# A transformer layer whose instruction order a planner writes: new durations and due times in the plan

## The chip, the core and the metric

The kernel runs on one core of one Trainium2 chip, in float32. Times are device microseconds (us) from the start of the program to its end. The profiler records one execution; its span goes from the first to the last instruction.

## What is computed

Eight sequences of 256 tokens with 512 features go through one layer. It normalises each token, runs causal attention with 32 query heads over 8 key/value heads of width 128 (so that 4 query heads share a key/value head), and multiplies the result by a gate from four small experts of which the best two count:

```python
xn = _layernorm(x)
q, k, v = heads of xn @ wq.T, xn @ wk.T, xn @ wv.T     # 32, 8 and 8 heads of 128
q, k = rotated by position                             # q * cos + rotate_half(q) * sin
scores = q @ k.T / sqrt(128)
scores = scores * scale        # for queries from position 107 on: 0.5 for keys under 35, 1.5 up to 107
probs = softmax(scores + causal)
s = (probs @ v) @ wo.T
g = silu(sum over the two best experts of gate * (xn @ A.T) @ B.T * 4)
return x + s * g
```

## The kernel before

**Blocks of work.** The tokens are cut into 4 token blocks (tb) of two sequences. Each block takes 8 steps, one for each key/value head with its 4 query heads (g). A step has two *units*, one for each sequence (b). A unit is one softmax: 4 heads x 256 queries x 256 keys.

The large products are done in Strassen-Winograd form: seven products of half matrices (pieces p1 to p7, four matmuls each) instead of eight, with sums and differences on VectorE before and after. `quad` makes the queries, keys and values in this way (TensorE tiles pa, pd, pe), `out_project` the output product (po). `out_project`'s left factors are the attention tiles a and their sums s; its results are added into acc by VectorE.

**A unit, link by link** (`softmax`, L681, and `values`, L806). TensorE writes the scores in three groups of query rows, 7-6, 5-4-3 and 2-1-0 (tiles sc). VectorE reduces each row to its least negated score (z, least). ScalarE takes the exponentials and their sums (p, total), with p one single buffer for all units, which the transposes of the unit before set free. VectorE then takes the reciprocal and scales p in two jobs (`scale`), and transposes 32x32 blocks in two more (`transpose`, tile blocks). SP, which issues transfers, writes these blocks to DRAM with four transfers (`spread`, there<-blocks) and reads them back with one (`gather`, pT<-there), so that the probabilities lie transposed for TensorE. Only then can TensorE multiply them by the values (`values`, tiles av, 6 matmuls in two pieces), ScalarE copy av to a, and `out_project` go on. The values of a unit come one step after its scores (LAG_V = 2 units).

**Who sets the order.** Nothing in the program waits for a scheduler at run time: each engine works through its instructions in the order in which the Python code issues them, and waits where an input is late. That order comes from `Plan` (L170). Each job is declared with `add` (L181): its engine, a duration in us, the jobs it comes after, the buffers it opens and closes (`Hold`, `Room`), a due time relative to a TensorE piece (`near`), and a `lag` for what passes until a transfer lands. TensorE's pieces are laid in a row by `lay` (L191), in the order that the loop at the end of `layer` (L1165 on) writes out. `Plan.run` (L195) gives every other job a due time: from `near`, or earlier where a job that needs it is due earlier. It then walks through its own clock. Whenever an engine is free by that clock, it takes the job with the earliest due time among those whose inputs are ready and whose buffers are free, and issues it; the job counts as done after its duration, the `lag`, and `HOP` (L175) for the signal. TensorE's pieces too are taken in this way: one that isn't ready by the plan's clock is passed by a later one. So a duration in the plan never makes an instruction longer or shorter; it moves instructions against each other.

**The start and the last steps.** `norm` (L309) loads four tiles of x per token block and finds mean and variance on VectorE (st, mv), the root on ScalarE and the reciprocal on VectorE (rstd), the normalised tile on VectorE (xn), its transpose on TensorE (xp) and a copy on ScalarE (XB). Weights come through GpSimd's queue (w, wo); in the first token block VectorE makes their sums, which are kept in DRAM for the later blocks. In the step loop each step's pieces are two lists, `fill` and `later`: scores and values of unit 0 and 1 (sa, va, sb, vb), and the output pieces of the step before (ob) and those held back from the one before that (oa). When no projection is left to weave in (the last steps), `fill + later` is laid as it stands.

Of the kernel before, what the change touches and what calls it, by code (L numbers as in the profile page):

```python
# [63 lines left out]
MIX = (SYS + IMG) // BLK  # L64
# [105 lines left out]
class Plan:  # L170
# [3 lines left out]

    HOP = 0.1  # L175
    AHEAD = 30.0
# [80 lines left out]
def layer(ctx: ExitStack, tc: tile.TileContext, x, wquad, woquad, raT, bT, table, out):  # L257
    nc = InOrder(tc)
# [50 lines left out]
    def norm(tb):  # L309
# [61 lines left out]
        for t in range(NT):  # L371
# [4 lines left out]
        loads = [  # L376
            add("dma", 0.0, lambda: None, after=[issues[t]], lag=6.0 if tb else 3.0 + 1.7 * t)
            for t in range(NT)
# [10 lines left out]
        for t in range(NT):  # L389
            xn = add("dve", 0.4, lambda t=t: normalise(t), after=[done[t]], opens=[mh[t]], closes=[xh[t // 2]])  # L390
            tp = add("pe", 0.5, lambda t=t: turn(t), after=[xn, identity], opens=[ph[t]], closes=[mh[t]])
            opens = [x_hold[tb]] if t == 0 else []
            after = [tp] + reads[:1]
            reads.append(
                add("act", 0.6, lambda t=t: read(t), after=after, opens=opens, closes=[ph[t]],
                    near=(tp, 0.5))
            )
            pieces.append(tp)
        t1 = add("dve", 0.7, lambda: add_up(0), after=reads)
        t2 = add("dve", 0.7, lambda: add_up(1), after=[t1])  # L400
        t3 = add("dve", 0.7, lambda: add_up(2), after=reads)
        t4 = add("dve", 0.7, lambda: add_up(3), after=[t2])
        acts[tb, "B"], acts[tb, "T"] = reads, [t1, t2, t3, t4]
# [4 lines left out]
    def blocks_of(tb, room, ring, source, kept, key, form, first):  # L408
# [26 lines left out]
        if tb:  # L435
            for i in order:
                after = [sums_of[room, key, i]] if i in form.sums else []
                there[i] = add("pool", 0.8, lambda i=i: load(i), after=after, opens=[holds[i]], lag=4.5)
            return box, holds, there
        issue = list(first)  # L440
        for i in order[:4]:
            there[i] = add(
                "sp" if first else "pool", 0.4 if first else 0.8, lambda i=i: load(i), after=issue,
                opens=[holds[i]], lag=10.0 if first else 4.5,
            )
        for i, (to, a, b, op) in enumerate(form.steps):
            there[to] = add(
                "dve", 0.7, lambda i=i: sum_up(i), after=[there[a], there[b]] + form.before(i, there),
                opens=[holds[to]] if to in order[4:] else [], closes=[holds[a], holds[b]],
            )  # L450
# [35 lines left out]
    def quad(tb, which, out, room, rows, name):  # L486
# [43 lines left out]
        def copy(what, p, h):  # L530
            return add(
                "act", 0.6, lambda: aside(what, "pa"), after=[p], opens=[h], near=(p, 0.0)
            )
# [5 lines left out]
        if not tb:  # L539
# [4 lines left out]
        o00 = add(  # L544
            "dve", 0.7, lambda: sum_up(0, 0, "pe", "p1"), after=[p2, c1], opens=[outs[0]],
            closes=[pe, s1], near=(p2, 1.0),
# [6 lines left out]
        o11 = add(  # L553
            "dve", 0.7, lambda: sum_up(1, 1, "pd", "u3"), after=[p5, c7], opens=[outs[1]],
            closes=[s3], near=(p7, 1.0),
        )
        p4 = piece("pa", A22, 0, 0, 3, False, [c7])
        o01 = add(
            "act", 0.6, lambda: nc.scalar.copy(out(0, 1), box["pa"]), after=[p4, o00],
            closes=[pa], near=(p4, 0.0),  # L560
        )
        p3 = piece("pd", S4, 1, 1, None, False, [o11])
        o10 = add(
            "dve", 0.7, lambda: sum_up(1, 0, "pd", "u2"), after=[p3, c6], closes=[pd, s2],
            near=(p3, 1.0),
# [3 lines left out]
    def rope(src, of, dst, opens, after, name):  # L569
# [21 lines left out]
        def turn():  # L591
            nc.vector.tensor_mul(split(box["sw"]), split(box["sw"]), wide(C_SIN))

        s0 = add("act", 1.05, lambda: swap(0), after=after, opens=[h], closes=[of])
        s1 = add("act", 1.05, lambda: swap(1), after=[s0], closes=[of])
        c = add(
            "dve", 1.22, lambda: nc.vector.tensor_mul(dst(), split(src()), wide(C_COS)),
            after=after + [tables], opens=opens, closes=[of],
        )
        t = add("dve", 1.22, turn, after=[s1])  # L600
        return add(
            "dve", 1.22, lambda: nc.vector.tensor_add(dst(), dst(), split(box["sw"])),
            after=[c, t], closes=[h],
# [12 lines left out]
    def keys_of(tb, half):  # L616

        pieces, outs, done, src = turned_quad(tb, KQ + half, f"k{tb}_{half}")

        def of(b):  # L620
            n = f"k{tb}_{half}_{b}"
            h, box = hold("kk"), {}

            def dst():
                if not box:
                    box["k"] = three.tile([P, G, 3, P], F32, tag="kk", name=f"k{n}")
                return box["k"][:, :, ::2, :]
# [9 lines left out]
            keys[tb, half, b] = box, h, add("dve", 0.7, rescale, after=[r])  # L637

        for b in range(NB):
            of(b)  # L640
        return pieces
# [39 lines left out]
    def softmax(tb, g, b):  # L681
# [93 lines left out]
        for rows in groups:  # L775
# [5 lines left out]
            red = add(  # L781
                "dve", sum(0.12 + 0.035 * (i + 1) for i in rows) + 0.3 * (MIX in rows),
                lambda r=rows: reduce(r), after=[sc], opens=[zh], closes=[sh], near=(sc, 1.0),
            )
            exps.append(
                add("act", sum(0.47 + 0.024 * (i + 1) for i in rows),
                    lambda r=rows: exponentials(r), after=[red, cleared] + exps[:1], closes=[zh],
# [15 lines left out]
        probs[tb, g, b] = box, th, in_  # L803
        return pieces

    def values(tb, g, b):  # L806
# [6 lines left out]
        def of(k):  # L813
# [18 lines left out]
            av = add("pe", 1.3, work, after=[p_done] + v_done, opens=[h], closes=[ph, vh])  # L832
            a = add("act", 0.6, read, after=[av], opens=[ah], closes=[h], near=(av, 1.0))
            attn[tb, g, b, k] = box, ah, a
# [6 lines left out]
    def out_project(tb, g):  # L841
# [19 lines left out]
        for i, (to, a, b, op) in enumerate(Features.steps):  # L861
            a_done[to] = add(
                "dve", 0.7, lambda i=i: sum_up(i),
                after=[a_done[a], a_done[b]] + Features.before(i, a_done),
# [4 lines left out]
        def product(k, a, w):  # L869
# [27 lines left out]
            mine["done"] = add(  # L897
                "act" if g == 0 else "dve", 0.7, add_up, after=[p, mine["done"]], closes=[h],
                opens=[mine["hold"]] if g == 0 else [], near=(p, 1.0),
# [17 lines left out]
    def finish(tb):  # L917
        M = {k: acc[tb, k] for k in range(1, 8)}

        def put(to, a, b, closes=()):  # L920
            near = max((M[a]["last"], M[b]["last"]), key=lambda p: p.number)
            M[to]["done"] = add(
                "dve", 0.7, lambda: nc.vector.tensor_add(M[to]["s"], M[a]["s"], M[b]["s"]),
                after=turn + [M[to]["done"], M[a]["done"], M[b]["done"]], closes=[M[k]["hold"] for k in closes],
# [8 lines left out]
        def inputs(b):  # L933
# [6 lines left out]
            def load(what):  # L940
# [6 lines left out]
                add("sp", 0.3, lambda: load("g"), after=gates[tb][2 * b : 2 * b + 2], opens=[xh],  # L947
                    near=near, lag=5.0),
                add("sp", 0.3, lambda: load("xf"), opens=[gh], near=near, lag=5.0),
            ]  # L950
            loads[b] = box, [xh, gh], done

        def result(k, b, f):
# [5 lines left out]
            m = add(  # L959
                "dve", 0.7, lambda: nc.vector.scalar_tensor_tensor(  # L960
                    s(), s(), 0.5, box["g"][:, :, cols], op0=ALU.mult, op1=ALU.mult
# [3 lines left out]
            a = add(  # L965
                "dve", 0.7, lambda: nc.vector.tensor_add(s(), s(), box["xf"][:, :, cols]),
                after=[m, done[1]], closes=[holds[1]], near=(near, 4.0),
# [22 lines left out]
    def experts(tb):  # L990
# [73 lines left out]
        p2 = add("pe", 0.5, turn, after=[r3], opens=[th])  # L1064
        last = add("act", 0.6, read, after=[p2], closes=[th], near=(p2, 0.5))

        def silu(t):
# [20 lines left out]
            p = add("pe", 0.86, work, after=[last], opens=[dh])  # L1088
            a = add("act", 0.6, half, after=[p], opens=[h], near=(p, 1.0))
            d = add("dve", 0.7, whole, after=[a], closes=[dh], near=(p, 2.0))  # L1090
            gates[tb].append(
# [73 lines left out]
    for n in range(len(steps) + 2):  # L1165
# [9 lines left out]
        if not last:  # L1175
# [51 lines left out]
```

## Time and profile before

| | |
|---|---|
| median of 3 runs | 1392.16 us (1383.55 to 1392.40) |
| profiled execution | 1394.26 us |
| its span | 1391.5 us |
| TensorE busy | 1340.2 us, 96% of the span |
| TensorE's weight loads | 1175.7 us, 84% |
| VectorE busy | 1102.4 us, 79% |
| ScalarE busy | 614.2 us, 44% |
| GpSimd busy | 313.8 us, 23% |
| moved by DMA | 275.8 MB, 198 GB/s mean |

PE is TensorE, DVE VectorE, ACT ScalarE, POOL GpSimd, SP SyncE; a q behind the name is the engine's queue, where transfers are issued. Names are the program's tiles, out<-in. The matmuls' ends are modelled by the profiler, so "busy" doesn't mean that TensorE is at its peak. In the view of waits a row gives who waited for whom, the us in total, how often, and the longest. In the timeline a row gives the start and the length in us, what ran and how often; in brackets, how long the engine was idle before it and what ended that. In the view by stretches a row gives the stretch, its length, the busy us of TensorE, of its weight loads, of VectorE, ScalarE and GpSimd (each with its number of instructions), the granted TensorE clock as a share of full speed, the share of DMA engines' time, and GB/s. Every line number is L118, since all instructions go through one recording helper; groups are told apart by their tiles.

### The profile page before, as it was taken

The numbers are of one execution on the slowest core, as the hardware profiler recorded it, in microseconds if no ns is written. First come the engines' busy times: TensorE is split into PE (matmuls) and PEld (weight loads), VectorE is DVE, ScalarE is ACT, GpSimd is POOL, SyncE is SP. The second block draws the span as 40 slices with busy tenths as digits, with TensorE's granted clock in tenths as the row PEclk, the third lists the DMA queues.
The fourth block names the chain that finished last, engine by engine and source line by source line (L and its number), as shares of the span: only waits on it lengthen the run. The fifth ranks groups of instructions, "written<-read, shape, count | busy, mean of one in ns | idle before, by whom it ended". The sixth has DMA issues, their size and how long they took to land.

```text
span 1391.5 us, 19888 instructions
## 1 busy us (share of the span) xinstructions
PE 1340.2 (96%) x6512; PEld 1175.7 (84%) x6512; DVE 1102.4 (79%) x2822; ACT 614.2 (44%) x1587; POOL 313.8 (23%) x579
## 2 busy tenths in 40 slices
PE   6999999999999999999999999999999999999985
PEld 5878888887888888888889888888878988888874
DVE  4897889898887868679687886868868877776885
ACT  2555444443544435345434554445543454444420
POOL 1422323222222122221222212212122121221110
PEclk9999999999999999999999999999999999999998
DMA  4676766666756666676667666666556586664672
GB/s 152 196 224 206 238 195 224 208 226 180 239 179 206 208 201 190 196 233 182 199 181 226 205 197 192 200 206 217 176 179 203 176 251 188 189 212 152 195 214 86
DMA packets 106134, 275.80 MB, mean 198 GB/s; under 512 B 15985, under 2 KB 52849, under 8 KB 106033
## 3 DMA queue, kind: packets, MB, share of 16 engines
q0 software_dynamic: 45760, 149.98, 34.7%
q1 hardware_dynamic: 59520, 123.76, 28.7%
q8 instruction: 52, 0.85, 0.2%
q10 hardware_dynamic: 752, 0.80, 0.2%
q14 instruction: 50, 0.40, 0.1%
HBM read 194.79 MB, written 79.69 MB: 197 GB/s over the span
## 4 chain that ended last, share of the span: by engine, by line
PE 83%; DMA 10%; DVE 4%; SPq 1%; issue 1%; ACT 0%; DVEq 0%; ACTq 0%
PE po L118 23%; PE paq L118 13%; PE av L118 11%; PE sc L118 9%; PE pdq L118 7%; DMA pT<-there 6%; PE pak L118 4%; PE pav L118 4%; DMA there<-blocks 4%; PE peq L118 3%; PE pdk L118 2%; PE pdv L118 2%; DVE acc L118 1%; PE dle L118 1%; PE pev L118 1%; PE lme L118 1%
## 5 line engine op out<-in xcount | busy, mean ns | idle before, releaser
L118 ACT ACTIVATE p<-z,least 128x256 f32<-128x256 f32 (+7 forms) x512 | 207.5, 407 | 110.6 <-DVE least L118 75.3
L118 PE MATMUL po<-wo,a 128*128 128x256 f32 x1024 | 241.2, 380 | 1.4 <-ACT a L118 1.4
L118 PE MATMUL av<-pT,v 128*128 128x256 f32 x768 | 194.1, 393 | 25.3 <-DMA pT<-there 25.3
L118 PEld LDWEIGHTS po<-wo,a 128*128 128x128 f32 x1024 | 192.2, 190 | 26.0 <-ACT a L118 2.6
L118 DVE CUSTOM_DVE_ANT_0 z<-sc,tab 128x256 f32<-128x256 f32 (+7 forms) x512 | 135.5, 301 | 78.8 <-PE sc L118 70.9
L118 PEld LDWEIGHTS av<-pT,v 128*128 128x128 f32 x768 | 149.5, 197 | 50.7 <-issue 14.4
L118 PE MATMUL po<-wo,s 128*128 128x256 f32 x768 | 182.7, 382 | 0.0
L118 PE MATMUL paq<-XT,w 128*128 128x256 f32 x768 | 182.0, 380 | 0.0
L118 PEld LDWEIGHTS sc<-kk,qTq 128*128 128x128 f32 x1024 | 159.9, 191 | 13.4 <-DVE least L118 1.0
L118 PE MATMUL sc<-kk,qTq 128*128 128x256 f32 (+7 forms) x1024 | 169.0, 303 | 1.3 <-DVE least L118 0.8
L118 DVE TENSOR_TENSOR acc<-acc,po 128x512 f32<-128x512 f32 x196 | 132.9, 678 | 46.7 <-PE po L118 44.8
L118 ACT COPY a<-av 128x512 f32<-128x512 f32 x128 | 73.9, 581 | 213.0 <-PE av L118 213.0
L118 PEld LDWEIGHTS po<-wo,s 128*128 128x128 f32 x768 | 145.2, 191 | 24.1 <-issue 5.3
L118 PEld LDWEIGHTS paq<-XT,w 128*128 128x128 f32 x768 | 144.8, 190 | 20.5 <-ACT p L118 0.8
L118 POOL DMA_DIRECT2D w<-sums x144 | 78.9, 548 | 361.0 <-PE paq L118 139.3
L118 ACT COPY swq<-cq 64x1024 f32<-64x1024 f32 x128 | 133.7, 1044 | 28.8 <-DVE qTq L118 22.7
L118 POOL DMA_DIRECT2D w<-in_wquad_dram x148 | 81.0, 549 | 252.4 <-PE paq L118 87.8
L118 DVE STREAM_TRANSPOSE blocks<-p 128x1024 f32<-128x1024 f32 (+1 forms) x128 | 123.5, 967 | 0.2
L118 DVE TENSOR_SCALAR p<-p,total 128x256 f32<-128x256 f32 (+7 forms) x512 | 118.1, 293 | 2.3
L118 ACT ACTIVATION_READ_ACCUMULATOR p<-z,least 128x1 f32 x512 | 96.1, 188 | 0.0
L118 DVE TENSOR_TENSOR qTq<-cq,tab 128x1024 f32<-128x1024 f32 x64 | 77.9, 1218 | 22.9 <-ACT cq L118 22.9
L118 POOL DMA_DIRECT2D wo<-osums x96 | 52.5, 546 | 152.5 <-PE po L118 152.5
(116 smaller groups left out, 1832.5 us busy)
## 6 DMA issues: line engine op xcount, KB each, us to landing
there<-blocks SPq DMA_DIRECT2D x256, 192.0 KB, 3.6
pT<-there SPq DMA_DIRECT2D x64, 768.0 KB, 5.7
w<-in_wquad_dram POOLq DMA_DIRECT2D x148, 256.0 KB, 4.7
w<-sums POOLq DMA_DIRECT2D x144, 256.0 KB, 3.8
wo<-in_woquad_dram POOLq DMA_DIRECT2D x104, 256.0 KB, 4.4
wo<-osums POOLq DMA_DIRECT2D x96, 256.0 KB, 4.2
sums<-w POOLq DMA_DIRECT2D x48, 256.0 KB, 3.6
osums<-wo POOLq DMA_DIRECT2D x32, 256.0 KB, 4.7
```

Source lines behind the costliest of these rows:

```text
L118: ins = what(*args, **kwargs)
```

## The change

The durations in the plan are set to new values, the due times of scaling, transposes and spread move nearer to the unit's last score piece, and the last step's pieces are laid in another order. No instruction is added, removed or altered. The same replacements as below are made wherever the old values stand: VectorE's sums 0.7 to 0.61, ScalarE's copies 0.6 to 0.5.

```diff
-    HOP = 0.1
+    HOP = 0.18
...
-            add("dma", 0.0, lambda: None, after=[issues[t]], lag=6.0 if tb else 3.0 + 1.7 * t)
+            add("dma", 0.0, lambda: None, after=[issues[t]], lag=8.5 if tb else 5.0 + 1.3 * t)
...
-                there[i] = add("pool", 0.8, lambda i=i: load(i), after=after, opens=[holds[i]], lag=4.5)
+                there[i] = add("pool", 0.8, lambda i=i: load(i), after=after, opens=[holds[i]], lag=6.0)
...
-        t = add("dve", 1.22, turn, after=[s1])
+        t = add("dve", 1.14, turn, after=[s1])
...
-                "dve", sum(0.12 + 0.035 * (i + 1) for i in rows) + 0.3 * (MIX in rows),
+                "dve", sum(0.06 + 0.033 * (i + 1) for i in rows) + 0.45 * (MIX in rows),
...
-                add("act", sum(0.47 + 0.024 * (i + 1) for i in rows),
+                add("act", sum(0.285 + 0.027 * (i + 1) for i in rows),
...
-        s0 = add("dve", 1.2, lambda: scale((7, 6, 5)), after=exps, near=(sc, 5.0))
-        s1 = add("dve", 0.9, lambda: scale((4, 3, 2, 1, 0)), after=[s0], near=(sc, 6.0))
+        s0 = add("dve", 0.95, lambda: scale((7, 6, 5)), after=exps, near=(sc, 3.0))
+        s1 = add("dve", 0.92, lambda: scale((4, 3, 2, 1, 0)), after=[s0], near=(sc, 3.5))
         t0 = add(
-            "dve", 1.24, lambda: transpose(False), after=[s1], opens=[bh], closes=[ph],
-            near=(sc, 7.0),
+            "dve", 1.17, lambda: transpose(False), after=[s1], opens=[bh], closes=[ph],
+            near=(sc, 4.0),
         )
         t1 = add(
-            "dve", 0.66, lambda: transpose(True), after=[t0], closes=[ph], near=(sc, 8.0)
+            "dve", 0.6, lambda: transpose(True), after=[t0], closes=[ph], near=(sc, 4.5)
         )
-        out_ = add("sp", 1.4, spread, after=[t1], closes=[bh], near=(sc, 9.0), lag=4.0)
-        in_ = add("sp", 0.35, gather, after=[out_], opens=[th], lag=5.0)
+        out_ = add("sp", 2.4, spread, after=[t1], closes=[bh], near=(sc, 5.0), lag=3.4)
+        in_ = add("sp", 0.35, gather, after=[out_], opens=[th], lag=7.0)
...
-                    near=near, lag=5.0),
-                add("sp", 0.3, lambda: load("xf"), opens=[gh], near=near, lag=5.0),
+                    near=near, lag=9.0),
+                add("sp", 0.3, lambda: load("xf"), opens=[gh], near=near, lag=9.0),
...
         later = [piece for some in later for piece in some]
+        if n == len(steps) - 1:
+
+            fill, later = sa + sb, oa + va + vb + ob[:2]
         main = []
```

More of the change, by code (lines that the diff above doesn't have):

```diff
@@ L394, in norm @@
             reads.append(
-                add("act", 0.6, lambda t=t: read(t), after=after, opens=opens, closes=[ph[t]],
+                add("act", 0.5, lambda t=t: read(t), after=after, opens=opens, closes=[ph[t]],
                     near=(tp, 0.5))
@@ L398, in norm @@
             pieces.append(tp)
[L399 to L402, printed above, removed]
+        t1 = add("dve", 0.61, lambda: add_up(0), after=reads)
+        t2 = add("dve", 0.61, lambda: add_up(1), after=[t1])
+        t3 = add("dve", 0.61, lambda: add_up(2), after=reads)
+        t4 = add("dve", 0.61, lambda: add_up(3), after=[t2])
         acts[tb, "B"], acts[tb, "T"] = reads, [t1, t2, t3, t4]
@@ L443, in blocks_of @@
                 "sp" if first else "pool", 0.4 if first else 0.8, lambda i=i: load(i), after=issue,
-                opens=[holds[i]], lag=10.0 if first else 4.5,
+                opens=[holds[i]], lag=10.0 if first else 6.0,
             )
@@ L447, in blocks_of @@
             there[to] = add(
-                "dve", 0.7, lambda i=i: sum_up(i), after=[there[a], there[b]] + form.before(i, there),
+                "dve", 0.61, lambda i=i: sum_up(i), after=[there[a], there[b]] + form.before(i, there),
                 opens=[holds[to]] if to in order[4:] else [], closes=[holds[a], holds[b]],
@@ L531, in copy @@
             return add(
-                "act", 0.6, lambda: aside(what, "pa"), after=[p], opens=[h], near=(p, 0.0)
+                "act", 0.5, lambda: aside(what, "pa"), after=[p], opens=[h], near=(p, 0.0)
             )
@@ L544, in quad @@
         o00 = add(
-            "dve", 0.7, lambda: sum_up(0, 0, "pe", "p1"), after=[p2, c1], opens=[outs[0]],
+            "dve", 0.61, lambda: sum_up(0, 0, "pe", "p1"), after=[p2, c1], opens=[outs[0]],
             closes=[pe, s1], near=(p2, 1.0),
@@ L553, in quad @@
         o11 = add(
-            "dve", 0.7, lambda: sum_up(1, 1, "pd", "u3"), after=[p5, c7], opens=[outs[1]],
+            "dve", 0.61, lambda: sum_up(1, 1, "pd", "u3"), after=[p5, c7], opens=[outs[1]],
             closes=[s3], near=(p7, 1.0),
@@ L558, in quad @@
         o01 = add(
-            "act", 0.6, lambda: nc.scalar.copy(out(0, 1), box["pa"]), after=[p4, o00],
+            "act", 0.5, lambda: nc.scalar.copy(out(0, 1), box["pa"]), after=[p4, o00],
             closes=[pa], near=(p4, 0.0),
@@ L563, in quad @@
         o10 = add(
-            "dve", 0.7, lambda: sum_up(1, 0, "pd", "u2"), after=[p3, c6], closes=[pd, s2],
+            "dve", 0.61, lambda: sum_up(1, 0, "pd", "u2"), after=[p3, c6], closes=[pd, s2],
             near=(p3, 1.0),
@@ L592, in turn @@
             nc.vector.tensor_mul(split(box["sw"]), split(box["sw"]), wide(C_SIN))
-        s0 = add("act", 1.05, lambda: swap(0), after=after, opens=[h], closes=[of])
-        s1 = add("act", 1.05, lambda: swap(1), after=[s0], closes=[of])
+        s0 = add("act", 1.0, lambda: swap(0), after=after, opens=[h], closes=[of])
+        s1 = add("act", 1.0, lambda: swap(1), after=[s0], closes=[of])
         c = add(
-            "dve", 1.22, lambda: nc.vector.tensor_mul(dst(), split(src()), wide(C_COS)),
+            "dve", 1.14, lambda: nc.vector.tensor_mul(dst(), split(src()), wide(C_COS)),
             after=after + [tables], opens=opens, closes=[of],
         )
-        t = add("dve", 1.22, turn, after=[s1])
+        t = add("dve", 1.14, turn, after=[s1])
         return add(
-            "dve", 1.22, lambda: nc.vector.tensor_add(dst(), dst(), split(box["sw"])),
+            "dve", 1.14, lambda: nc.vector.tensor_add(dst(), dst(), split(box["sw"])),
             after=[c, t], closes=[h],
@@ L636, in of @@
             r = rope(lambda: src[b], outs[b], dst, [h], done[b], n)
-            keys[tb, half, b] = box, h, add("dve", 0.7, rescale, after=[r])
+            keys[tb, half, b] = box, h, add("dve", 0.61, rescale, after=[r])
         for b in range(NB):
@@ L832, in of @@
             av = add("pe", 1.3, work, after=[p_done] + v_done, opens=[h], closes=[ph, vh])
-            a = add("act", 0.6, read, after=[av], opens=[ah], closes=[h], near=(av, 1.0))
+            a = add("act", 0.5, read, after=[av], opens=[ah], closes=[h], near=(av, 1.0))
             attn[tb, g, b, k] = box, ah, a
@@ L862, in out_project @@
             a_done[to] = add(
-                "dve", 0.7, lambda i=i: sum_up(i),
+                "dve", 0.61, lambda i=i: sum_up(i),
                 after=[a_done[a], a_done[b]] + Features.before(i, a_done),
@@ L897, in product @@
             mine["done"] = add(
-                "act" if g == 0 else "dve", 0.7, add_up, after=[p, mine["done"]], closes=[h],
+                "act" if g == 0 else "dve", 0.61, add_up, after=[p, mine["done"]], closes=[h],
                 opens=[mine["hold"]] if g == 0 else [], near=(p, 1.0),
@@ L922, in put @@
             M[to]["done"] = add(
-                "dve", 0.7, lambda: nc.vector.tensor_add(M[to]["s"], M[a]["s"], M[b]["s"]),
+                "dve", 0.61, lambda: nc.vector.tensor_add(M[to]["s"], M[a]["s"], M[b]["s"]),
                 after=turn + [M[to]["done"], M[a]["done"], M[b]["done"]], closes=[M[k]["hold"] for k in closes],
@@ L959, in result @@
             m = add(
-                "dve", 0.7, lambda: nc.vector.scalar_tensor_tensor(
+                "dve", 0.61, lambda: nc.vector.scalar_tensor_tensor(
                     s(), s(), 0.5, box["g"][:, :, cols], op0=ALU.mult, op1=ALU.mult
@@ L965, in result @@
             a = add(
-                "dve", 0.7, lambda: nc.vector.tensor_add(s(), s(), box["xf"][:, :, cols]),
+                "dve", 0.61, lambda: nc.vector.tensor_add(s(), s(), box["xf"][:, :, cols]),
                 after=[m, done[1]], closes=[holds[1]], near=(near, 4.0),
@@ L1064, in experts @@
         p2 = add("pe", 0.5, turn, after=[r3], opens=[th])
-        last = add("act", 0.6, read, after=[p2], closes=[th], near=(p2, 0.5))
+        last = add("act", 0.5, read, after=[p2], closes=[th], near=(p2, 0.5))
         def silu(t):
@@ L1088, in silu @@
             p = add("pe", 0.86, work, after=[last], opens=[dh])
-            a = add("act", 0.6, half, after=[p], opens=[h], near=(p, 1.0))
-            d = add("dve", 0.7, whole, after=[a], closes=[dh], near=(p, 2.0))
+            a = add("act", 0.5, half, after=[p], opens=[h], near=(p, 1.0))
+            d = add("dve", 0.61, whole, after=[a], closes=[dh], near=(p, 2.0))
             gates[tb].append(
```

## The prediction

> **What bounds the kernel now.** I read the chain of work that ended last first, for the engine that sets the end; then the waits, for what TensorE lacks; then the stretches around single waits, for what a wait costs after it is over; then the timelines of one late softmax, for which step made it late.
>
> ```profile
> PE 83%; DMA 10%; DVE 4%; SPq 1%; issue 1%; ACT 0%; DVEq 0%; ACTq 0%
> ```
>
> TensorE sets the end. The 10% of DMA is 6% gathers of the turned probabilities (pT<-there) and 4% spreads of their blocks: the last links of softmax, which TensorE waits for before it can multiply by the values. The waits:
>
> ```profile
> PE av L118 <- DMA pT<-there: 25.3, 13, 3.6
> ...
> PE xp L118 <- DVE xn L118: 12.8, 4, 8.0
> ...
> DVE total L118 <- ACT p L118: 3.9, 5, 0.9
> ...
> PE po L118 <- ACT a L118: 1.4, 2, 0.7
> ```
>
> Columns: total us, times, longest. TensorE is idle for 41.2 us inside the span: 25.3 us for pT, 12.8 us at the start, 3.1 us of small ones. After TensorE's last product 10.1 us follow (acc, output). VectorE is busy for 79% and has room. A long wait costs more than itself:
>
> ```profile
> 692.80:695.20 2.40, 0.04 (x2) 0.05 (x1) 2.40 (x10) 2.08 (x10) 1.09 (x2) 1.00 0.99 404
> 695.20:698.60 3.40, 3.40 (x16) 3.01 (x17) 0.63 (x2) 1.76 (x2) 0.00 (x0) 1.00 0.75 278
> 1030.00:1033.00 3.00, 0.04 (x1) 0.07 (x1) 2.86 (x10) 2.68 (x10) 1.08 (x2) 0.96 1.01 406
> 1033.00:1036.10 3.10, 3.10 (x8) 2.47 (x9) 0.00 (x0) 1.11 (x2) 0.00 (x0) 0.50 0.68 258
> ```
>
> The third number from the end is the granted clock. After 2.36 us of idling it stays 1.00; after 2.99 us it is 0.50 for 3.4 us, in which TensorE does half its work: 1.7 us more. The same follows the waits that end at 318.9, 1343.7 and 1367.3 us; after the one that ends at 105.0 us the 0.50 lasts 6.8 us (3.4 us lost). Together 10.2 us. DMA is full (0.99, 1.01) just before two of these waits.
>
> Why softmax is late, shown by the unit (two per step: one key/value group of one sequence) whose av starts at 105.0 us:
>
> ```profile
> 78.41 0.18 DVE L118 CUSTOM_DVE_ANT_0 z<-sc,tab 128x32 f32<-128x32 f32 x1
> ...
> 78.52 0.69 DVE L118 TENSOR_TENSOR w<-w,w 128x512 f32<-128x512 f32 x1
> 79.12 1.22 DVE L118 TENSOR_TENSOR qTq<-cq,tab 128x1024 f32<-128x1024 f32 x1
> 80.26 1.22 DVE L118 TENSOR_TENSOR swq<-swq,tab 128x1024 f32<-128x1024 f32 x1
> ...
> 83.73 0.19 DVE L118 RECIPROCAL total<-total 128x8 f32<-128x8 f32 x1
> ...
> 90.00 0.71 DVE L118 STREAM_TRANSPOSE blocks<-p 128x512 f32<-128x512 f32 x1
> ```
>
> ```profile
> 90.74 2.23 SPq L118 DMA_DIRECT2D there<-blocks  x4
> ...
> 97.79 0.34 SPq L118 DMA_DIRECT2D pT<-there  x1
> ```
>
> ScalarE's exponentials end at 80.4, but the reciprocal waits until 83.7 behind w and query work that was put ahead of it, and 7.0 us pass to the end of the transposes, which with reciprocal and scaling need only 3.7 (start to start: 0.23+1.66+1.16+0.63). Spread 7.0 us, gather 7.2 us, av at 105.0. Over all 64 units the spread takes 4.8 to 8.5 us (mean 6.1), the gather 4.1 to 7.6 (mean 5.7), both from issue to landing.
>
> **The change, part by part.** Every engine has the same instructions before and after (8180 in all): nothing is added or removed, only the order moves. So all effects are waits.
>
> Durations. From 78.52 to 79.12 us is 0.60, not the plan's 0.7; 79.12 to 80.26 is 1.14, not 1.22: the new values are start-to-start times of such rows. The spread gets 2.4+3.4 instead of 1.4+4.0, the gather 0.35+7.0 instead of 0.35+5.0, 1.6 above its mean: on the late side, so TensorE's next work is put ahead of an av rather than behind it.
>
> The mid waits, one by one. In the changed order I count the products between a unit's last score and its first av (1.73 us each by the timeline), and the VectorE work between its last reduction and last transpose (start to start). Where av starts (us): wait; TensorE work gained; VectorE work taken out of the chain. 105.0: 3.60; 1.7; 2.3. 318.9: 2.93; 0.8; 3.5. 450.1: 1.04; 0; 1.1. 620.3: 0.60; 1.7; 0.3. 695.2: 2.36; 5.2; 0.6. 786.0: 1.52; 0; 1.1. 913.2: 0.74; 0; 2.9. 957.4: 1.05; 1.7; 0.3. 1033.0: 2.99; 5.2; 0.6. 1125.2: 1.29; 0; 1.1. 1252.6: 1.06; 0; 2.9. Waits 19.2 us, halved clock 6.8 us (3.4+1.7+1.7). The two gains together cover each wait but 0.6 us; in the unit after those at 450, 786 and 1125 the chain grows by 1.2 us, against 2.3 to 3.2 us of slack that shrinks by the wait removed: 0.5 us. Mid gain 26.0-1.1 = 24.9.
>
> [...] The rows show it after 2.57, 2.93 and 2.99 us too, so I take the 10.2[...].
>
> The tail. The last step's scores are put ahead (new lines 1188 to 1190). Its last scores move from 1301.3 to 1296.6 us of TensorE work, its last unit gets 22.1 us of products before av instead of 17.3. Also ScalarE: before, that unit's exponentials stand behind the copies of the preceding av, which waits for pT, so its first exponential runs at 1347.2; now they stand ahead. The second load of x leaves the place between spread and gather of the unit at 1343.7, whose gather took 7.0 us (4.3 at its neighbours), and goes ahead of the preceding gather, whose unit has 2.8 us of cover. Before: 0.79+2.57+0.72+3.58+0.68 = 8.3 of waiting, 3.4 of clock. After: the two 0.7 us waits for an a copy stay, and with exponentials 3.3, transposes done 4.3 later, spread 5.3 and gather 4.5 (their rows in this stretch) the last two av come about 0.5 us late each: 2.4. Gain 9.3.
>
> The start. Reciprocals sit idle for ScalarE's root (0.98, 0.92, 0.92 us before 9.8, 12.5, 15.2 us), because ScalarE's root stands behind the copy of the transposed tile. Now the next tile's statistics fill this, and two roots stand ahead of the first copy. x lands at 5.7, 6.6, 8.7 and 9.7 us, so following the new order by row durations xn ends at 8.6, 10.3, 12.3 and 13.3 instead of 7.8 to 16.1 us: 2.7 us off the last, of which the slow first products (pak 2.66 us instead of 1.73) may give back 1.4. Between +1 (first tile late) and -2.7: I take -2.0.
>
> What is moved back. VectorE does about 5 us more work by the same point of TensorE's first token block (weight sums and query work pulled ahead as shorter), so some s, xn and query tiles now stand behind it. Shift against TensorE minus slack, summed over the five places where it is worst (s: 7.8 against 2.4, 6.3 against 1.6 three times; xn: 7.3 against 0.7), gives 26 us if VectorE were never idle there, and 0 if its idle time (2.5 to 7 us of each 35) takes it up, as the shorter durations say. No row shows the new order; below zero has no reason. I take 5, nearer the end that the 0.60 and 1.14 us rows support, and keep 0 to 26. The issues of SP are the same 394 instructions, in nearly the same order; SP waits only for the last transpose, which comes earlier.
>
> Sum: -24.9-9.3-2.0+5 = -31.2. The profiled execution has span 1391.5 and own time 1394.3, so 1360.3 and 1363.1; it lies 2.1 above the median 1392.2, so 1361 in the median.
>
> **Rivals.** *Landings bind (1374).* The waits come with full DMA; an earlier transpose may meet the same weight loads, and land no earlier. Then only TensorE work moved ahead counts: of the mid waits 1.7+0.8+0.6+2.4+1.1+3.0 = 9.6 and 1.7 of clock, half the tail 4.7, the start 2: -18. For it: spread 7.0 to 8.4 us at late units, 4.8 at others. Against: the weights load when TensorE frees their buffers, not by the transposes.
>
> *VectorE becomes the wait (1382).* The full 26 us appear instead of 5: -10.2. For it: 32.5 of 35 us busy at 245 to 315. Against: PE waits for DVE after the start sum to 1.6 us now, and the new durations agree with the rows.
>
> *Order on a strict queue (1420).* The scalings now stand about 2 us earlier. [...] This speaks against the change. Row: DVE total<-ACT p, 3.9 us in 5 waits of 64, the longest 0.9. At 1 us per unit it costs 64 against 36.2 gained: +28, so 1420. Slower than before from 0.6 us per unit on. Against: the plan now gives eight exponentials 3.3 us, as the rows have it start to start.
>
> **How the numbers follow.** Forecast 0.57 (own range 1353 to 1370), landings 0.22, VectorE 0.14, strict queue 0.07. About 1% is what a measurement of this kernel can tell from no change: 13.9 us, 1378.2 and 1406.1. Faster: 0.57 + nearly all of 0.22 + a quarter of 0.14 = 0.81; slower: 0.05, most of the strict queue; same: the rest, 0.14. Range 1351 to 1379: the floor is all waits gone (1391.5-28.4-10.2-2.7 = 1350 in the span), the top takes in the landings case.
>
> **What would show it.** Right: pT waits under 6 us in fewer places, no 0.50 clock in mid-kernel, reciprocals close behind the exponentials, first pak before 16 us. Wrong: pT waits at the same places with spreads of 7 us and more (landings); PE waits for xn, s or qTq of several us before 320 us (VectorE); DVE total<-ACT p beyond 40 us (strict queue).

## The result, and the profile after

| | before | after |
|---|---|---|
| median (lowest to highest), 4 runs each | 1392.28 us (1383.55 to 1392.92) | 1370.59 us (1366.63 to 1372.18) |
| ratio, with its 95% interval | | 0.9854 (0.981 to 0.9899) |
| profiled execution, its span | 1394.26, 1391.5 us | 1371.18, 1369.4 us |
| TensorE idle inside the span | 41.2 us | 25.0 us |
| half of the time at the half clock, up to the last product | 10.2 us | 3.4 us |
| after TensorE's last product | 10.1 us | 10.1 us |

The kernel is 1.5% faster: 21.7 us in the median, where 31 were forecast. The chain that ended last, of after:

```profile
PE 83%; DVE 8%; DMA 7%; issue 1%; SPq 0%; ACT 0%; DVEq 0%
```

DMA's share went from 10% to 7%. That VectorE has 8% now and had 4% says less: the chain follows one path back, and where two paths are nearly as late it takes one of them. The waits of after:

```profile
PE av L118 <- DMA pT<-there: 10.4, 9, 3.4
...
DVE total L118 <- ACT p L118: 9.4, 12, 1.7
...
PE xp L118 <- DVE rstd L118: 8.6, 2, 8.0
...
DVE blocks L118 <- DMA there<-blocks: 3.1, 1, 3.1
...
PE po L118 <- DVE s L118: 2.7, 1, 2.7
```

TensorE waits for pT in 9 places for 10.4 us, against 13 places and 25.3 us. Seven of the nine are in the middle (8.4 us, before 19.2): 1.44 us at 114.2, 0.16 at 395, 1.34 at 438.1, 0.30 at 727.8, 3.35 at 772.7, 0.23 at 1065 and 1.62 at 1108.4. The three of 1.34, 3.35 and 1.62 us are the same units as the waits at 450.1, 786.0 and 1125.2 before: the first unit of the second step of token blocks 1 to 3. Of the list in the prediction these three stayed and the other eight went; the wait at 114.2 is of another unit than the one that waited at 105.0: the first of the second step in token block 0. The longest, by stretches:

```profile
769.30:772.70 3.40, 0.05 (x2) 0.04 (x1) 2.82 (x9) 0.59 (x1) 1.08 (x2) 0.87 1.02 393
772.70:778.60 5.90, 5.90 (x14) 4.85 (x15) 3.78 (x9) 0.59 (x1) 0.00 (x0) 0.50 0.47 168
```

TensorE does nothing for 3.4 us while the DMA engines are full (1.02), and then has the half clock (0.50), from 771.8 to 778.6 us. It is the only halved stretch left before TensorE's last product.

At the start, the first product of after against 16 us before which it was to come:

```profile
11.85 0.55 DVE L118 TENSOR_SCALAR xn<-x,mv,rstd 128x512 f32<-128x512 f32 x1
```

```profile
13.36 3.62 PE L118 MATMUL pak<-XB,w 128*128 128x256 f32 x8
16.77 2.23 PE L118 MATMUL pek<-XB,w 128*128 128x256 f32 x8
```

It begins at 13.4 us (17.0 before), but its eight matmuls take 3.62 us and the next eight 2.23.

The sum, term by term, from idle time and clock:

| | forecast gain | measured gain | of it waits, clock, other |
|---|---|---|---|
| middle | 24.9 | 14.2 | 10.8, 3.4, 0 |
| last two steps | 9.3 | 4.6 | 1.2, 3.4, 0 |
| start | 2.0 | 2.6 | 3.7, 0, -1.1 (slow first products) |
| VectorE moved back | -5 | 0.5 | other small waits, 0.9 to 0.4 |
| sum | 31.2 | 21.9 | the span: 22.1 |

### The profile page after: what moved, and what is told of

It reads as the page before. It is cut to its first block, busy times and chain, and to the rows that moved or that the text cites. A ratio compares the mean times of both kernels' runs of the same rounds, so it can differ in the third digit from the quotient of the medians.

```text
span 1369.4 us, 19896 instructions
## 1 busy us (share of the span) xinstructions
PE 1334.2 (97%) x6512; PEld 1171.1 (86%) x6512; DVE 1096.7 (80%) x2822; ACT 618.0 (45%) x1587; POOL 314.4 (23%) x579
## 4 chain that ended last, share of the span: by engine, by line
PE 83%; DVE 8%; DMA 7%; issue 1%; SPq 0%; ACT 0%; DVEq 0%
PE po L118 24%; PE paq L118 14%; PE av L118 11%; PE sc L118 9%; PE pdq L118 7%; DMA pT<-there 5%; PE pak L118 4%; PE peq L118 3%; PE pav L118 3%; PE pdk L118 2%; DMA there<-blocks 2%; PE pdv L118 1%; DVE blocks L118 1%; PE dle L118 1%; DVE acc L118 1%; PE lme L118 1%
## 5 line engine op out<-in xcount | busy, mean ns | idle before, releaser
L118 PE MATMUL av<-pT,v 128*128 128x256 f32 x768 | 186.9, 382 | 10.4 <-DMA pT<-there 10.4
L118 PEld LDWEIGHTS av<-pT,v 128*128 128x128 f32 x768 | 145.3, 191 | 32.7 <-issue 7.5
L118 PEld LDWEIGHTS sc<-kk,qTq 128*128 128x128 f32 x1024 | 159.3, 191 | 13.4 <-issue 0.8
```

Source lines behind the costliest of these rows:

```text
L118: ins = what(*args, **kwargs)
```

## The experiments

Before any of them the theory was the prediction's: the waits for pT go because the plan's numbers put the softmax's VectorE work earlier and TensorE's other work ahead of av. Its rivals were that the due times alone do it, that the transfers' durations alone do it, and that the landings, not the order, set what is left. Ratios are to the kernel before in the same runs; the kernel before had medians of 1389.14, 1390.46 and 1388.77 us in the three groups.

### Which part of the change carries the gain

**Due times alone.** In before, the five due times as the change has them:

```diff
-        s0 = add("dve", 1.2, lambda: scale((7, 6, 5)), after=exps, near=(sc, 5.0))
-        s1 = add("dve", 0.9, lambda: scale((4, 3, 2, 1, 0)), after=[s0], near=(sc, 6.0))
+        s0 = add("dve", 1.2, lambda: scale((7, 6, 5)), after=exps, near=(sc, 3.0))
+        s1 = add("dve", 0.9, lambda: scale((4, 3, 2, 1, 0)), after=[s0], near=(sc, 3.5))
...
-            near=(sc, 7.0),
+            near=(sc, 4.0),
```

> The kernel before with the five new due times alone (3.0, 3.5, 4.0, 4.5, 5.0 us behind the last score); durations, transfers and last step as before. If the dues bring the gain (the forecast gave them the VectorE work taken out of the chain), about a third to a half of it comes here: 1376 to 1385 us. If the order is made by the durations, and the dues only choose among jobs that the plan's clock already holds ready, nothing is gained: by the counted order the chain loses 0.6 us of VectorE work at the wait of 318.9 us and 2.3 at 105.0, while TensorE's work ahead of av shrinks by 1.7 us at 105.0, 450, 786 and 1125 us, so about 1392 to 1397 us with pT waits of 25 to 30 us.

Measured: 1388.14 us, ratio 0.9992 (0.9977 to 1.0006). Its waits, fewer than the 25 to 30 us that were expected:

```profile
PE av L118 <- DMA pT<-there: 20.3, 12, 3.3
```

Twelve waits are left, and the clock is halved three times (mean granted clock 0.994, in before 0.990). The due times alone are worth nothing that can be measured.

**The last step's order alone**, in before: the three new lines at 1188 to 1190.

> The kernel before with the last step's order alone. If the new order works by itself, the tail's waits fall from 11.7 us with halved clock to about 3 to 7 us: 1383 to 1388 us, mid waits unchanged at 19 us. If it needs the new durations to help, 1390 to 1394 us.

Measured: 1387.05 us, 0.9987 (0.997 to 1.0004). The scores that are put ahead now wait themselves, 0.70 and 3.37 us at 1321 to 1326 us, both until VectorE has reduced earlier scores (least). No gain either.

**The transfers' durations alone**, in before:

```diff
-        out_ = add("sp", 1.4, spread, after=[t1], closes=[bh], near=(sc, 9.0), lag=4.0)
-        in_ = add("sp", 0.35, gather, after=[out_], opens=[th], lag=5.0)
+        out_ = add("sp", 2.4, spread, after=[t1], closes=[bh], near=(sc, 9.0), lag=3.4)
+        in_ = add("sp", 0.35, gather, after=[out_], opens=[th], lag=7.0)
...
-                    near=near, lag=5.0),
-                add("sp", 0.3, lambda: load("xf"), opens=[gh], near=near, lag=5.0),
+                    near=near, lag=9.0),
+                add("sp", 0.3, lambda: load("xf"), opens=[gh], near=near, lag=9.0),
```

and the loads of x, w and wo likewise.

> The kernel before with the new transfer durations alone (spread 2.4+3.4, gather 0.35+7.0, weight loads 6.0, x loads, g and xf 9.0). By the counted order TensorE's work ahead of av grows by 1.7 to 5.2 us at every one of the eleven mid waits (2.5 at 450, 786 and 1125), more than each wait. If what TensorE does in the meantime decides, the mid waits (19.2 us) and their halved clock (6.8 us) go, tail and start stay (1392-26 = 1366 us). If the shorter VectorE and ScalarE durations decide, little happens: 1385 to 1392 us.

Measured: 1368.23 us, 0.984 (0.9815 to 0.9864). Its waits:

```profile
PE av L118 <- DMA pT<-there: 4.6, 4, 2.3
```

As fast as the whole change, though its softmax is no quicker: from the last scores to pT a unit takes 23.15 us in the mean of 64, against 23.0 before and 21.7 after. What grew is the work that TensorE has ahead of av: pT now lies there 5.4 us before its av in the mean, against 4.6.

**All durations, old due times, old last step** (the change less those two parts; one more new value is among them than "The change" lists, ScalarE's swaps of the query's halves, 1.05 to 1.0). The first due time stands at 9.0 in this kernel instead of the old 5.0, which gives the same order of all jobs.

> The changed kernel without its new due times and without its last-step order: all new durations alone. If the dues matter little, mid and start are as in the changed kernel (16.8 us gained there) and only the tail differs: 1371 to 1377 us. If the dues carry their part of the chain, the pT waits come back above 15 us: 1380 to 1385 us.

Measured: 1367.23 us, 0.9837 (0.981 to 0.9864). With the two tests above: neither due times nor last step add to the gain.

**The change with the old transfers' durations** (the edit of transfers, undone in after).

> The changed kernel with the old durations of all transfers: dues, engine durations, HOP and the last step's order are the new ones. Against the kernel before (1389), VectorE work leaves the chain as in the changed kernel (0.2 to 3.5 us at the mid waits), but TensorE has no more ahead of av, at two waits 1.7 us less. If the VectorE work counts in full, as the forecast's sum had it, the mid waits fall from 19 to about 12 us and their clock returns in part; with the start (2.6) and the tail (4.6) 1370 to 1375 us. If earlier transposes land no earlier, and only TensorE work ahead removes a wait, the mid stays and start and tail alone come: 1380 to 1385 us.

Measured: 1374.39 us, 0.9875 (0.9828 to 0.9922). Its waits:

```profile
PE av L118 <- DMA pT<-there: 9.3, 7, 2.4
```

So the other road works as well: here the chain is 21.3 us, 1.7 shorter than before, TensorE's order ahead of av at the three units is the old one, and most waits go too. By the medians the two roads give 21 and 16 us alone and 22 together; they remove the same waits and don't add up.

**One number.** In before, only this:

```diff
-        in_ = add("sp", 0.35, gather, after=[out_], opens=[th], lag=5.0)
+        in_ = add("sp", 0.35, gather, after=[out_], opens=[th], lag=7.0)
```

> The kernel before with one number changed: the gather is planned at 0.35+7.0 us instead of 0.35+5.0. By the counted order TensorE's work ahead of av grows by 1.7 to 5.2 us at ten of the eleven mid waits (not at 105.0 us), VectorE's order stays nearly as it was. If this one number carries the mid gain, nearly all of what the transfers' values together gave (1368) comes: 1368 to 1374 us, with the wait at 105 us and those of the tail left. If the spread or the loads share it, 1376 to 1384 us.

Measured: 1364.88 us (1363.82 to 1365.47), 0.9826 (0.9788 to 0.9865), with no halved clock in the middle (mean granted clock 0.997, in after 0.995). Its waits:

```profile
PE av L118 <- DMA pT<-there: 4.1, 5, 1.7
```

The median lies 5.7 us under that of the whole change, by the ratios 3.9 us (0.0028 of 1390); the two intervals overlap. One number is enough for the whole gain. Why the rest of the change adds nothing to it is seen at the unit whose av waits at 1108.4 us in after. First after, then this kernel, TensorE's timeline:

```profile
1103.20 1.89 PE L118 MATMUL peq<-XB,w 128*128 128x256 f32 x8
1104.93 1.89 PE L118 MATMUL po<-wo,s 128*128 128x256 f32 x8
1108.44 1.53 PE L118 MATMUL av<-pT,v 128*128 128x256 f32 x6 [1.62 <-DMA pT<-there]
```

```profile
1099.96 1.89 PE L118 MATMUL peq<-XB,w 128*128 128x256 f32 x8
1101.69 1.89 PE L118 MATMUL po<-wo,s 128*128 128x256 f32 x8
1103.42 0.97 PE L118 MATMUL sc<-kk,qTq 128*128 128x256 f32 x4
1104.23 1.89 PE L118 MATMUL po<-wo,s 128*128 128x256 f32 x8
1105.96 1.46 PE L118 MATMUL av<-pT,v 128*128 128x256 f32 x6
```

The same products in both, then a scores piece and an output piece more (0.81 + 1.73 = 2.5 us start to start) ahead of av, and no wait. With the long gather in its clock the plan found av not ready and passed it. In after, with the same gather but shorter VectorE and ScalarE durations, av was issued at once, as in before. That is because pT was there by the plan's clock. Worked out from the two programs, and counted from the start of the unit's last scores, it has pT ready at 23.4 us in after, just before TensorE comes free for av at 23.7. In this kernel pT is ready at 24.8, so that two pieces go first and av at 26.3.

### What keeps the three waits

In these units the gather takes 8.1, 8.6 and 8.6 us in after, against 7.3, 6.9 and 7.6 before; the chain of after has the last one:

```profile
1099.70 8.61 DMA pT<-there
```

The spread before it takes 7.3, 8.7 and 7.0 us (6.3, 7.2 and 6.3 before). SP's queue at this unit, before, then after:

```profile
1117.41 0.34 SPq L118 DMA_DIRECT2D pT<-there  x1
1117.79 0.43 SPq L118 DMA_DIRECT2D g<-gates  x1
```

```profile
1098.19 0.34 SPq L118 DMA_DIRECT2D g<-gates  x1
1099.70 0.34 SPq L118 DMA_DIRECT2D pT<-there  x1
1100.08 0.43 SPq L118 DMA_DIRECT2D xf<-in_x_dram  x1
```

The 512 KB load of the gates (g) now goes 1.5 us ahead of the 768 KB gather; at the two other units 1.7 and 3.2 us ahead, where before it stood 0.4 us behind. The test puts it, and the second load of x (xf), behind this gather, in after:

```diff
...
+        if (g, b) == (1, 0) and tb:
+            for job in second[tb - 1]:
+                in_.then.append(job)
+                job.waits += 1
...
```

> The changed kernel with one more dependency in the plan: the second g and xf load of a token block (512 KB each) come after the gather of the first unit of the next block's second step, which they now stand in front of (g) or right behind (xf). If these loads lengthen that gather (8.1, 8.6, 8.6 us in the changed kernel, 6.0 mean over all units), it falls to about 6 us and the pT waits at 438, 773 and 1108 us (1.34, 3.35, 1.62, and 3.4 of halved clock) go: 6 to 9 us less than the changed kernel, 1362 to 1365 us. If the weight loads on GpSimd's queue are what fills the engines there, the gathers stay above 7.5 us and the time within 3 us of the changed kernel's 1370.

SP's queue of this kernel at the same unit:

```profile
1093.34 0.34 SPq L118 DMA_DIRECT2D pT<-there  x1
1093.72 0.43 SPq L118 DMA_DIRECT2D out_dram<-acc  x1
1094.20 0.85 SPq L118 DMA_DIRECT2D g<-gates  x1
```

The three gathers take 7.6, 6.4 and 7.4 us, their waits go from 1.34, 3.35 and 1.62 to 0.46, 1.14 and 0.35, and the halved clock is gone (mean granted clock 0.998, in after 0.995). So the loads at this place lengthened the gathers, which took 8.1, 8.6 and 8.6 us in after. Time of this kernel: 1368.35 us (1363.17 to 1369.18), 0.9824 (0.9783 to 0.9865); the profiled execution gained 8 us, the median 2, and the intervals overlap with after's: the mechanism is shown in the trace, its worth in the median is not.

**The gather's duration 9.5 instead of 7.0**, in after: TensorE work ahead of av again, where after has none.

> The changed kernel with the gather planned at 0.35+9.5 us instead of 0.35+7.0. By the counted order TensorE's work ahead of av grows by 2.5 us or more at nearly all even units (at 438, 773 and 1108 us too), VectorE's order hardly changes. If TensorE work ahead of av is what removes a wait, all three remaining mid waits go (6.3 us and 3.4 of clock): 1360 to 1364 us. If a later av only moves the wait (to a buffer, an a copy or the tail), 1368 us or more.

Measured: 1357.90 us (1357.30 to 1359.64), 0.9759 (0.9722 to 0.9796). Its waits:

```profile
PE av L118 <- DMA pT<-there: 0.5, 1, 0.5
```

Every pT wait in the middle is gone, though the three gathers still take 8.3, 7.8 and 7.0 us. Late landings don't bind as such; what they need is cover.

**Duration 9.5 with old due times and old last step** (the kernel of all durations above, its 9.0 too, with this number).

> All new durations with the gather at 0.35+9.5 us, but the old due times and the old last step. If the dues add nothing, as the run of dues alone said, the middle is as without waits as with them, and only the tail can differ: 1355 to 1361 us. If they help once the middle is clear, 1363 us or more.

Measured: 1358.88 us, 0.9784 (0.9738 to 0.9831): within 1 us of longer. Due times and last step add nothing here either.

**Duration 12.0**, in after.

> The changed kernel with the gather at 0.35+12.0 us, twice what it takes (6.0 mean). If a later av costs nothing while other products are at hand, the time stays at 1356 to 1360 us, as with 9.5. If it begins to hold buffers of the probabilities or push work to the end, 1361 us or more.

Measured: 1359.33 us (1358.90 to 1362.40), 0.9792 (0.9752 to 0.9832). Once the cover is there, more of it brings nothing and costs little.

### The wait in the last step

VectorE's timeline of after, in the last step:

```profile
1326.55 0.20 DVE L118 RECIPROCAL total<-total 128x8 f32<-128x8 f32 x1 [1.71 <-ACT p L118]
1326.79 1.75 DVE L118 TENSOR_SCALAR p<-p,total 128x256 f32<-128x256 f32 x8
1331.62 1.25 DVE L118 STREAM_TRANSPOSE blocks<-p 128x1024 f32<-128x1024 f32 x1 [3.09 <-DMA there<-blocks]
1332.79 0.65 DVE L118 TENSOR_TENSOR s<-a,a 128x512 f32<-128x512 f32 x1
```

and TensorE's:

```profile
1333.49 3.72 PE L118 MATMUL po<-wo,s 128*128 128x256 f32 x16 [2.67 <-DVE s L118]
```

The transposes of the last unit can't start until the spread of the unit before has left blocks, of which there is one buffer. The sums s are issued behind them on VectorE, and po waits for s. The test takes the last unit's blocks from the buffers of the keys, in after:

```diff
...
-                box["blocks"] = one.tile([P, NQ, 3 * P], F32, tag="blocks", name=f"blocks{n}")
+                box["blocks"] = (three if ends else one).tile(
+                    [P, NQ, 3 * P], F32, tag="kk" if ends else "blocks", name=f"blocks{n}"
+                )
...
```

> The changed kernel in which the last unit's transposed blocks go to a free buffer of the same size (one of the three for keys) instead of the one buffer that the unit before still reads from. If VectorE's wait for that buffer (3.1 us, until the spread of the unit before has landed) is what holds up s and so the output products (2.67 us at 1330.8 us), both go: 2 to 4 us less than the changed kernel's 1370. If TensorE then waits for the last pT instead, nothing is gained.

Measured: 1369.52 us (1364.17 to 1372.48), 0.9836 (0.9792 to 0.988). Both waits are gone, and another has their place:

```profile
1339.70 2.83 PE L118 MATMUL av<-pT,v 128*128 128x256 f32 x12 [1.92 <-DMA pT<-there]
```

This is the av of the unit before, whose spread took 8.1 us (1325.04 to 1333.16, from the issue to that of the gather) and its gather 6.5 (to 1339.70). The wait for s had covered it.

**All three together**: duration 9.5, gather first, the second blocks buffer.

> The changed kernel with the gather at 0.35+9.5 us, the second g and xf load after the gather, and the last unit's blocks in a buffer of their own. The mid waits are gone already with 9.5 alone (1357.9); what is left is the start (9.6 us of idling) and the tail. If the last buffer's wait (2.8 us before s) can be had now that pT comes 5 us early there, and 1.7 us of halved clock with it: 1353 to 1356 us. If a pT wait takes its place, as in the kernel with the buffer alone: 1357 to 1359 us.

Measured: 1354.48 us (1354.22 to 1355.34), 0.9754 (0.9716 to 0.9791): the lowest median here. By the ratios that is 14 us under the change. TensorE is idle for 13.4 us in it, 9.2 of it at the start. Against the duration 9.5 alone (0.9759, from another group of runs) the two other edits show no gain that can be measured by the ratios. In the profiled executions the wait for s fell from 2.80 to 1.26 us and the 3.4 us of half clock behind it went.

## Why the prediction was right, and where not

The measured 1370.6 us lies between the forecast (1361) and the landings case (1374): inside the range given (1351 to 1379), just outside the forecast's own (1353 to 1370). That it is so near owes something to luck: of 15.4 us missed in the middle and the tail, 5.5 came back because the cost set aside for VectorE did not appear.

**Right: what is lost and why.** TensorE's waits for pT and the halved clock after them were the loss, and a new order removed most of both. Eight of eleven listed waits went, from the end of the start to 320 us TensorE has no wait for xn, s or qTq, the reciprocal starts 0.6 us behind the last exponential in the mean (1.8 before), and the first product comes before 16 us. Two of the signs named did not come: the pT waits are 10.4 us, not under 6, and one stretch of half clock is left in the middle.

**Wrong: "The two gains together cover each wait but 0.6 us."** This is the step that failed, for 10.7 us (24.9 forecast, 14.2 measured), 9.1 of them in the three units whose waits stayed. There the cover was to be VectorE's work alone (0 us of TensorE, 1.1 of VectorE). That part came: from the end of the last reduction to the end of the last transpose 8.7 became 7.3 us. But spread and gather of the same units took 0.7 to 1.5 and 0.8 to 1.7 us longer, so nothing was left for TensorE. This is what the landings rival said, but it held only in units where VectorE's work was the whole cover: in the kernel with the old transfers' durations shorter VectorE work removed most waits. The gather's part of the lengthening comes from the order of two loads on SP's queue (7.6, 6.4 and 7.4 us with them behind, for 8.1, 8.6 and 8.6); why the spreads grew is open. I had written that SP's issues come in "nearly the same order"; the difference was just there. Worse, one wait grew to 3.35 us, and with the half clock after it (3.4 us) cost 6.8 us in all, where the forecast left 0.6 us to the three units together.

**Wrong in size: the tail** (9.3 forecast, 4.6 measured). The scores did move ahead, and 3.4 us of halved clock went. "Spread 5.3 and gather 4.5 (their rows in this stretch)" were 8.4 (1323.15 to 1331.60) and 6.2 (landed at 1337.77) for the last unit but one, 7.2 and 5.4 for the last. The av at 1325.3 waited 1.82 us and that at 1346.9 waited 0.17, where two waits of about 0.5 were forecast. The single blocks buffer, which turns a late spread into a stall of VectorE, isn't in the working at all; it came to 2.67 us of TensorE. And the last step's order, taken alone, gained nothing.

**Too high: VectorE moved back** (5 forecast, nothing measured). No such wait shows in the first token block; the low end, 0, was the right one. The VectorE wait that came (2.67 us) is counted in the tail.

**Right: the start**, 2.6 for 2.0 us. x landed at 5.08 us here, 5.71 in before, so 0.6 of it is the load's.

**The half clock.** The prediction took it as the rows of before have it: after waits of 2.57, 2.93 and 2.99 us as well as after those of 3.58 and 3.60. But in these traces the length of one wait doesn't tell whether it comes. With the due times alone, a wait of 3.25 us (ended at 779.4; the idle time of the first two rows) was followed by no half clock, and one of 1.93 us (ended at 1026.3, fourth row) by 3.4 us of it:

```profile
774.21:777.62 3.41, 1.95 (x10) 1.36 (x8) 1.55 (x2) 1.82 (x9) 0.55 (x1) 1.00 0.95 317
777.62:781.03 3.41, 1.62 (x8) 1.47 (x9) 0.00 (x0) 0.00 (x0) 0.00 (x0) 1.00 0.92 291
781.03:784.45 3.42, 3.42 (x18) 3.06 (x17) 2.01 (x4) 0.59 (x1) 1.09 (x2) 1.00 0.40 142
1023.38:1026.79 3.41, 1.48 (x8) 1.00 (x7) 3.38 (x12) 3.38 (x14) 1.09 (x2) 1.00 0.94 320
1026.79:1030.20 3.41, 3.41 (x10) 2.66 (x9) 0.81 (x3) 1.26 (x2) 0.00 (x0) 0.50 0.71 278
```

What a wait of 2 to 3.5 us costs beyond itself is therefore known only for those that were measured; what decides it was not shown. The forecast of the middle's clock held for the waits it counted: all 6.8 us of before's went, and the new 3.4 is the grown wait's.

**The strict queue.** DVE total<-ACT p, VectorE's waits for the exponentials of a unit that it is to scale, grew from 3.9 us in 5 waits to 9.4 in 12, 0.15 us per unit, far from the 0.6 from which it would decide. The fixed order on VectorE shows in one place: in the last step the sums s stand behind transposes that wait 3.09 us for the blocks.

**Not foreseen: which number does it.** The prediction called the gather's 7.0 the late side, "so TensorE's next work is put ahead of an av", and by its landings case let TensorE's work cover 9.6 of 19.2 us. Alone, that number brought the median down by 23.9 us; the rest of the change shortens the softmax by 1.0 us more in the mean (22.7 to 21.7, from the last scores to pT), and at the three units it goes with an av that is issued sooner. So the two roads, TensorE's other work and shorter VectorE work, work against each other in the plan: a softmax that is shorter by its clock takes away the pieces that it puts ahead of av. At five of the eleven listed waits after has no more TensorE work there than before, the kernel with the one number 2.5 to 3.5 us more.

**Open.** Over all units the spread went from 6.13 to 6.36 us and the gather from 5.67 to 6.03, of which the order of the two loads explains three units (with them put behind, the mean is still 6.05). The 1.4 us wait at 114.2 us was not tried separately; with the duration 9.5 it is gone. Whether the one number is better than the whole change needs more runs than the four of each.

## What to carry to other kernels

Where a plan decides which product goes next, the duration that it believes of a transfer is a margin: set it above the slowest landing (9.0 us in after) and the engine that bounds gets cover (1370.6 to 1357.9 us from 7.0 to 9.5); a duration near the mean leaves the late ones uncovered. When a plan's other durations are made shorter at the same time, look again at what they do to that margin. Before crediting a shorter chain, check per unit what stands between its end and the product that needs it, and follow the transfers on their queue too: they share it with loads that the new order may put ahead.

## What the runs showed of the hardware

In the three units above the 768 KB gather took 8.1, 8.6 and 8.6 us in after, where the 512 KB load of g was issued 1.5 to 3.2 us ahead of it on the same queue, and 7.6, 6.4 and 7.4 us in the kernel with the gather first, where this load and the second one of x came behind it. In before, with the load of g 0.4 us behind, it took 7.3, 6.9 and 7.6 us. Over all 14 traces it took 7.0 to 9.8 us (mean 8.5, 21 gathers) with the load of g issued 0.5 to 3.2 us ahead, and 6.1 to 8.3 us (mean 7.2, 21 gathers) with it 0.4 to 0.9 us behind. Only the kernel with the gather first was made to change the order of these loads alone.

The granted clock of TensorE was 0.50 for 6.8 us in before with the wait of 3.60 us and for 3.4 us each with those of 2.57, 2.93, 2.99 and 3.58 us, and it stayed 1.00 with that of 2.36 us. In after it was 0.50 for 6.8 us with the wait of 3.35 us. With the due times alone it stayed 1.00 with a wait of 3.25 us and was 0.50 for 3.4 us with one of 1.93 us.
